# Window scores of an attention layer: whole-array products against products on quarters of TensorE, with keys laid out by two multiplications

## The chip, the cores and the metric

The kernel runs on one core of a Trainium2 chip. The metric is device time in microseconds (us) of one launch. The core's engines are TensorE (PE; its weight loads are shown apart as PEld), VectorE (DVE), ScalarE (ACT), GpSimd (POOL) and SyncE (SP, which issues DMAs). They run side by side, each through its own list of instructions in order, and wait for one another by semaphores. PE writes its products to PSUM, which has eight banks of 128 partitions by 512 float32 values; DVE and ACT read them from there.

## The reference

16 images become 441 tokens each and get 128 text tokens appended, so there are 16 sequences of 569 tokens with 256 features. Layer 0 is an attention in windows of 64 tokens and a mixture of eight experts, layer 1 a phasor attention and an LSTM. Everything is float32. The change touches the window attention alone:

```python
    qkv = xw @ w_qkv.T + b_qkv
    qkv = qkv.reshape(b, w, p, 3, N_HEADS, HEAD_DIM)       # p = 64, 8 heads of 32
    ...
    sim = jnp.einsum('bwphd,bwqhd->bhwpq', q, k) * scale
    ...
    sim = sim + rel_pos[:, idx][None, :, None]
    ...
    probs = jax.nn.softmax(sim, axis=-1)
    out = jnp.einsum('bhwpq,bwqhd->bwphd', probs, v)
    ...
    out = out @ w_out.T + b_out
```

## The kernel before, in words

The program runs in stages. The first holds the tokenizer, the window attention, the norms and the routing of tokens to experts; then come the experts (line 1320 and on), layer 1 and the LSTM, and the output.

The first stage takes the sequences in eight pairs. A pair has nine chunks of 128 rows, each of two windows of 64 tokens (one window of each sequence), so there are 72 chunks. A chunk goes through `windows` (lines 716 to 836) in one of four slots, each slot with a PSUM bank and SBUF tiles of its own. Its steps are: turn the normalised rows (L724); project to queries and keys into the slot's bank, four blocks of 128x128 (L734); add the bias to the queries (L743); lay out the keys (L708); scores (L752); scale and add the relative position (L758); project the values and the gate (L768, L777); softmax (L782 to L803); turn the probabilities (L807); multiply by the values (L819); project out (L830); add to the residual (L832). Then `sent_rows` and `norm` write the normalised rows for the experts. Beside the windows run `features` and `projections` (the tokenizer's input), two slots of `tokens` (its attention, L611 to L652), `norms` (the norm ahead of the windows), and `routing`, which for each pair ranks the experts, counts places by a product with a triangular matrix (L893, L895, into bank 7), and forks `send`, POOL's indirect DMAs (L927). The last pair is routed in three parts: chunks 0 to 3, 4 to 6, and 7 and 8.

How the scores work: the projected keys have 128 partitions, four heads of 32 features each, in two groups m. To get separate scores per head from one product, the key tile `KB` is 128 partitions by 256 columns per window, with head r's keys in columns 64r to 64r + 63 of partitions 32r to 32r + 31 and zeros elsewhere (zeroed once, L445). Four copies per chunk fill in the diagonal blocks (L708: rows 0 and 1 by ACT, 2 and 3 by DVE). A product of 64 queries with 256 columns then gives four heads' scores. For the two windows w it writes the two halves of the output partitions, that is, it uses the array as two halves of 64 columns.

The order of the work is not left to a scheduler. Every step of these generators names its engine and an expected duration (`yield "PE", 0.44, "64"`), and `Order.run` merges the streams: it keeps a clock for each engine, and takes the step that could start earliest. A third entry "64" says that the step uses the array in 64-column tiles; going to another kind is charged. `yield "at", event` holds a stream until another has marked the event; `yield "lock", name` until no other stream holds that name; `first.fork` starts a new stream. The merged order is the order in each engine's list. So a changed duration can move any later instruction of the stage.

Of the kernel before, what the change touches and what calls it, by code (L numbers as in the profile page):

```python
# [297 lines left out]
def kernel(ctx: ExitStack, tc: tile.TileContext, a: dict, out: bass.AP):  # L298
# [121 lines left out]
    def setup():  # L420
# [22 lines left out]
        nc.gpsimd.memset(zeros, 0.0)  # L443
        for t in KB + VB:
            nc.gpsimd.memset(t, 0.0)  # L445
        for t in QT:
            nc.vector.memset(t, 0.0)
        nc.gpsimd.memset(ones, 1.0)
        nc.gpsimd.memset(before, 0.0)
        for e in range(1, E):  # L450
# [149 lines left out]
    def tokens(slot):  # L600

        last = NIMG - 384
        for n in range(slot, 7 * NP, 2):
# [4 lines left out]
            for m in range(2):  # L608
                yield "PE", 0.76, "64"
                for s in range(2):  # L610
                    nc.tensor.matmul(  # L611
                        sc[64 * s : 64 * s + 64, :NIMG], QT[s][:, m, 64 * c : 64 * c + 64],
                        fTs[2 * p + s][:, m, :], start=(m == 0), stop=(m == 1),
                    )
# [20 lines left out]
            for t in range(4):  # L635
                m = min(128, NIMG - 128 * t)
                yield "PE", 0.44, "64"
                for s in range(2):
                    nc.tensor.matmul(
                        mm[64 * s : 64 * s + 64, :], PT[:m, t, 64 * s : 64 * s + 64],  # L640
                        TV[s][:m, t, :], start=(t == 0), stop=(t == 3),
                    )
# [14 lines left out]
    def norm(h, to, name, slot):  # L657

        st = wk.tile([128, 6], F32, name=f"{name}_st", tag=f"st{slot}", bufs=1)
        yield "DVE", 0.43  # L660
        nc.vector.bn_stats(st, h[:, :D])
        mv = wk.tile([128, 2], F32, name=f"{name}_mv", tag=f"mv{slot}", bufs=1)
        yield "DVE", 0.18
        nc.vector.bn_aggr(mv, st)
        rstd = wk.tile([128, 1], F32, name=f"{name}_rstd", tag=f"rstd{slot}", bufs=1)
        yield "POOL", 0.85 if name[0] == "r" else 1.28
        over = mv[:, 1:2]
        nc.gpsimd.tensor_scalar(over, over, EPS, None, ALU.add)
        nc.gpsimd.tensor_tensor(rstd, over, mhalf[:, :1], ALU.pow)
        if name[0] == "w":  # L670
            nc.gpsimd.tensor_tensor(h[:, D + E :], over, half, ALU.pow)
        yield "DVE+", 0.5
        nc.vector.tensor_scalar(to, h[:, :D], mv[:, 0:1], rstd, ALU.subtract, ALU.mult)
        return rstd

    def norms():
# [10 lines left out]
    def sent_rows(p, c, h, slot):  # L687

        if p not in XN:
            if p > 1:  # L690
                yield "at", ("sent", p - 2)
            if p not in XN:
                LG[p] = wk.tile([128, NC, E], F32, name=f"LG{p}", tag="LG", bufs=2)
                XN[p] = xnp.tile([128, NC, WIDE], F32, name=f"XN{p}", tag="XN", bufs=2)
                yield "POOL", 0.2
                nc.gpsimd.tensor_copy(XN[p][:, :, D], cols[:, COL["row"] + NC * p : COL["row"] + NC * (p + 1)])
        rstd = yield from norm(h, XN[p][:, c, :D], f"r{p}_{c}", slot)
        yield "DVE", 0.19
        nc.vector.scalar_tensor_tensor(
            LG[p][:, c, :], h[:, D : D + E], rstd, frow("gate_b", E), ALU.mult, ALU.add  # L700
        )
        first.mark(("normed", p, c))

    def half_of_keys(u, kb, qk, rows, engine):
        for r in rows:
            own = slice(32 * r, 32 * r + 32)
            yield engine, 0.4
            (nc.scalar.copy if engine == "ACT" else nc.vector.tensor_copy)(  # L708
                kb[own, :, :, r, :], qk[own, 1].rearrange("p m (w x) -> p m w x", w=2)
            )  # L710
        first.mark(("keys", u, engine))

    def windows(slot):

        kb, vb = KB[slot], VB[slot]
        for n in range(slot, NC * NP, WINDOWS):
# [13 lines left out]
            for m in range(2):  # L730
                for j in range(2):
                    for k in range(2):
                        yield "PE", 0.25
                        nc.tensor.matmul(  # L734
                            qk[:, j, m, :], wqkv[:, k, D * j + 128 * m : D * j + 128 * m + 128],
                            xT[:, k, :], start=(k == 0), stop=(k == 1),
                        )
            q = wk.tile([128, 2, 128], F32, name=f"wq{u}", tag=f"wq{slot}", bufs=1)
            first.fork(half_of_keys(u, kb, qk, (0, 1), "ACT"))
            first.fork(half_of_keys(u, kb, qk, (2, 3), "DVE"))  # L740
            for m in range(2):
# [5 lines left out]
            yield "at", ("keys", u, "DVE")  # L747
            sc = place_of(f"wsc{u}", slot).rearrange("p (h x) -> p h x", h=NH)
            for m in range(2):
                yield "PE", 0.44, "64"  # L750
                for w in range(2):
                    nc.tensor.matmul(  # L752
                        sc[64 * w : 64 * w + 64, 4 * m : 4 * m + 4, :],
                        q[:, m, 64 * w : 64 * w + 64], kb[:, m, w, :, :], start=True, stop=True,
                    )
            S = wk.tile([128, NH, 64], F32, name=f"wS{u}", tag=f"wS{slot}", bufs=1)
            yield "DVE", 0.69
            nc.vector.scalar_tensor_tensor(  # L758
                S, sc, 32 ** -0.5, relm if c == 8 else rel, ALU.mult, ALU.add
            )  # L760

# [11 lines left out]
            for k in range(2):  # L773
                yield "PE", 0.06, "64"
                for w in range(2):
# [6 lines left out]
            nc.vector.tensor_reduce(top, S, AX.X, ALU.max)  # L782
            yield "DVE", 0.2
            nc.vector.scalar_tensor_tensor(
                h[:, D : D + E], vg[:, D : D + E], h[:, D + E :], win_b[:, D:], ALU.mult, ALU.add
            )
            for odd in range(2):
                own = slice(64 * odd, 64 * odd + 64)
                yield "ACT", 0.4
                nc.scalar.copy(  # L790
# [47 lines left out]
    def routing():  # L838

        for p, lo, hi in PARTS:  # L840
# [45 lines left out]
            for c in range(n):  # L886
                yield "DVE", 0.19
                nc.vector.tensor_tensor(
                    ahead[:, c + 1, :], ahead[:, c, :], both[:, c, :], ALU.add
                )  # L890
            pos = place_of(f"pos{u}", 7)[:, : (n + 1) * E].rearrange("p (c e) -> p c e", e=E)
            yield "PE", 0.3
# [8 lines left out]
            yield "DVE", 0.16  # L901
            nc.vector.tensor_tensor(place0, place0, pos[:, n:, :], ALU.add)
            part = wk.tile([128, 2, n, E], F32, name=f"part{u}", tag="part", bufs=1)
            for of, to in ((pr, share), (place, slot)):
# [32 lines left out]
    with tc.manual_schedule(engines=ENGINES):  # L937
# [8 lines left out]
        win_b = hp.tile([128, D + E], F32, name="win_b")  # L946
        half = hp.tile([128, 1], F32, name="half")
        mixed = hp.tile([128, NB, 2, len(EDGES)], F32, name="mixed")
        QT = [hp.tile([128, 2, 448], F32, name=f"tQ{s}") for s in range(2)]


        KB = [hp.tile([128, 2, 2, 4, 64], F32, name=f"KB{i}") for i in range(WINDOWS)]
        VB = [hp.tile([128, 2, 4, 2, 32], F32, name=f"VB{i}") for i in range(WINDOWS)]
# [1214 lines left out]
```

## Time and profile before

| | us |
|---|---|
| median of 3 runs | 3315.19 |
| lowest and highest run | 3311.05, 3320.17 |
| the profiled execution, its own time | 3305.14 |
| its span, from the first to the last instruction | 3303.4 |
| first score product of the first stage (L752) | starts 59.1 |
| first product of the experts (L1320) | starts 966.8 |

A row of the groups reads: line, engine, operation, output tile <- input tiles, partitions by elements, count | busy us, mean ns of one | idle us of the engine just before them, and what ended most of it. A row of the timeline reads: start, length, engine, line, operation, tiles, shape, count, and in brackets the idle time before it with its releaser. In a shape such as 128\*64 the first number is the rows of the array that a matmul uses and the second its columns; what follows are partitions and columns of the moving data. A float32 matmul of the program is two in the profile. PE's busy time overlaps within itself, as matmuls are pipelined and their ends are modelled; the distance between starts tells what one costs.

### The profile page before, as it was taken

The page shows a single profiled execution, that of the slowest core. Times are in us where ns is not written, and L with a number is a line of the kernel's source. Part 1 is how long each engine was busy: PE and PEld are TensorE (multiplying, and loading weights), DVE is VectorE, ACT ScalarE, POOL GpSimd, SP SyncE. Part 2 cuts the span into 40 slices and gives each one's busy share as a digit, 9 for nine tenths or more (in the row PEclk, how much of TensorE's full clock was granted, in tenths as well). Part 3 has the DMA queues.
Part 4 walks back from the last instruction along what each step waited for, and adds up shares of the span by engine and source line. Part 5 has one row for each costly group of instructions (what it writes and reads, how often), then busy time and mean ns, then how long its engine had stood idle before and what let it go on. Part 6 is the DMA issues. An engine that isn't in the chain of part 4 may idle for free.

```text
span 3303.4 us, 133968 instructions
## 1 busy us (share of the span) xinstructions
PE 2989.9 (91%) x57598; PEld 2205.3 (67%) x57598; DVE 2051.8 (62%) x6946; ACT 1486.8 (45%) x5068; POOL 815.6 (25%) x1579
## 2 busy tenths in 40 slices
PE   6999999999849999997899999999999999899884
PEld 3666666666638888885576767677676766666552
DVE  4678777786742222222676777677777777676555
ACT  3544544454412222222554556556665656454442
POOL 1354465545533332322311101010110010000000
PEclk8999999999979999998999999999999999999997
DMA  5111221101177676773433333333333333233323
GB/s 180 58 62 57 74 85 63 52 31 45 41 240 247 242 254 236 250 245 121 125 89 102 89 91 96 99 92 98 92 88 97 89 100 87 74 96 92 101 86 116
DMA packets 268419, 378.43 MB, mean 115 GB/s; under 512 B 133088, under 2 KB 207888, under 8 KB 255152
## 3 DMA queue, kind: packets, MB, share of 16 engines
q1 hardware_dynamic: 242192, 313.73, 30.1%
q0 software_dynamic: 14160, 38.83, 3.1%
q10 hardware_dynamic: 11472, 17.30, 1.8%
q8 instruction: 451, 7.39, 0.9%
q14 instruction: 144, 1.18, 0.1%
HBM read 252.06 MB, written 117.70 MB: 112 GB/s over the span
## 4 chain that ended last, share of the span: by engine, by line
PE 36%; DVE 7%; ACT 6%; DMA 2%; issue 2%; POOL 0%; SPq 0%; ACTq 0%; DVEq 0%; POOLq 0%
PE gates L1832 13%; PE xm_False L1116 6%; PE out_gate L1841 2%; PE v L1116 2%; ACT act L1853 1%; PE ek L1116 1%; PE eq L1116 1%; ACT th L1889 1%; DMA xo<-XOD 1%; PE r_False L1116 1%; DVE ab L1868 1%; PE po_False L1116 1%; DVE cT L1881 1%; PE ds_False L1116 1%; DVE act L1874 1%
## 5 line engine op out<-in xcount | busy, mean ns | idle before, releaser
L1832 PE MATMUL gates<-W_hh,X 128*16 128x96 f32 (+1 forms) x18176 | 490.8, 248 | 63.9 <-DVE X L1896 60.3
L1832 PEld LDWEIGHTS gates<-W_hh,X 128*16 128x16 f32 (+1 forms) x18176 | 378.3, 103 | 252.9 <-DVE X L1896 236.1
L1327 ACT ACTIVATE hT<-hp,w 128x256 f32<-128x256 f32 (+1 forms) x332 | 132.9, 453 | 448.8 <-PE hp L1320 342.0
L1853 ACT ACTIVATE act<-gates 128x96 f32<-128x96 f32 x568 | 142.1, 250 | 412.1 <-PE gates L1832 403.4
L1116 PE MATMUL xm_False<-W_ih,dxT_False 128*32 128x256 f32 x4352 | 294.3, 382 | 0.8 <-ACT dxT_False L1356 0.6
L1868 DVE SCALAR_TENSOR_TENSOR ab<-act 128x64 f32<-128x64 f32 x568 | 127.9, 225 | 255.6 <-ACT act L1853 248.5
L1334 PE MATMUL y<-w,hT 128*128 128x256 f32 x1208 | 276.3, 381 | 6.9 <-ACT hT L1327 6.8
L1340 DVE TENSOR_TENSOR ys<-y,w 128x512 f32<-128x512 f32 (+1 forms) x83 | 53.4, 644 | 358.5 <-PE y L1334 306.6
L1320 PE MATMUL hp<-xt,w 128*128 128x256 f32 (+1 forms) x1328 | 275.2, 360 | 0.0
L1775 PEld LDWEIGHTS <-nil 128*32 128x32 bf16 x4552 | 186.4, 95 | 119.0 <-issue 60.4
L1334 PEld LDWEIGHTS y<-w,hT 128*128 128x128 f32 x1208 | 226.3, 190 | 41.8 <-ACT hT L1327 11.8
L1320 PEld LDWEIGHTS hp<-xt,w 128*128 128x128 f32 x1328 | 232.8, 190 | 28.7 <-ACT hT L1327 0.2
L1261 POOL DMA_INDIRECT YT<-ys,to x151 | 147.3, 975 | 416.8 <-DVE ys L1340 389.6
L1841 PE MATMUL out_gate<-W_hh,X 128*32 128x64 f32 x9088 | 235.5, 220 | 6.1 <-issue 3.2
L1781 ACT COPY gates<-xc 128x96 f32<-128x96 f32 x569 | 138.6, 244 | 140.9 <-PE gates L1775 62.8
L1841 PEld LDWEIGHTS out_gate<-W_hh,X 128*32 128x32 f32 x9088 | 189.2, 111 | 11.0 <-issue 4.0
L1896 DVE SCALAR_TENSOR_TENSOR X<-toT,th 128x32 f32<-128x32 f32 x569 | 109.6, 193 | 129.2 <-ACT th L1889 126.3
L1889 ACT ACTIVATE th<-cT 128x32 f32<-128x32 f32 x569 | 130.4, 229 | 89.5 <-DVE cT L1881 49.0
L927 POOL DMA_INDIRECT XS<-XN,at x144 | 150.3, 1044 | 51.3 <-issue 24.6
L734 PE MATMUL wqk<-wxT,wqkv 128*128 128x128 f32 x1152 | 150.3, 280 | 7.6 <-ACT wxT L728 7.2
L734 PEld LDWEIGHTS wqk<-wxT,wqkv 128*128 128x128 f32 x1152 | 140.0, 192 | 24.1 <-ACT wxT L728 13.5
L1775 PE MATMUL gates<-nil 128*32 128x96 bf16 x2276 | 132.5, 209 | 24.2 <-ACT act L1853 4.5
(383 smaller groups left out, 6493.8 us busy)
## 6 DMA issues: line engine op xcount, KB each, us to landing
w<-in_wpack SPq DMA_DIRECT2D x83, 1154.0 KB
taps<-in_taps SPq DMA_DIRECT2D x16, 1764.0 KB
xc<-XCD SPq DMA_DIRECT2D x71, 384.0 KB
XCD<-xp_False SPq DMA_DIRECT2D x136, 192.0 KB
yg<-YT SPq DMA_DIRECT2D x72, 256.0 KB
xo<-XOD SPq DMA_DIRECT2D x71, 256.0 KB
xs<-XS SPq DMA_DIRECT2D x68, 258.0 KB
HD<-h SPq DMA_DIRECT2D x72, 128.0 KB
```

Source lines behind the costliest of these rows:

```text
L734: nc.tensor.matmul(qk[:, j, m, :], wqkv[:, k, D * j + 128 * m : D * j + 128 * m + 128], xT[:, k, :], start=(k == 0), stop=(k == 1),)
L927: fill(0, nc.gpsimd.indirect_dma_start(out=XS[0], out_offset=bass.IndirectOffsetOnAxis(ap=at[:, i, c - lo : c - lo + 1], axis=0), in_=XN[p ...
L1116: nc.tensor.matmul(out[own], lhsT[:, own], rhs, start=start, stop=stop)
L1261: keep(nc.gpsimd.indirect_dma_start(out=YT, out_offset=bass.IndirectOffsetOnAxis(ap=to[:, i : i + 1], axis=0), in_=ys[:, i, :], in_offset= ...
L1320: nc.tensor.matmul(hp[:, i, : 128 * n], w1[:, k, hc * 128 : (hc + 1) * 128], xT[:, k, :], start=(k == 0), stop=(k == 1),)
L1334: nc.tensor.matmul(y[:, i, :], hT[:, hc, 128 * i : 128 * i + 128], w2[:, hc, :], start=(hc == 0), stop=(hc == 3),)
L1775: nc.tensor.matmul(g[32 * q : 32 * q + 32, :n], nil[:, :32], nil[:, :n], start=True, stop=last)
L1832: nc.tensor.matmul(GC[32 * q : 32 * q + NB * (1 + half), :96], before[:, kk, NB * (1 - half) :], Whh[:, kk, own : own + 96], start=False, ...
L1841: nc.tensor.matmul(GO[32 * q : 32 * q + 32, :64], before[:, kk, :], Whh[:, kk, own : own + 64], start=False, stop=(kk == 1),)
L1853: nc.scalar.activation(act[:, :96], GC[:, :96], AF.Tanh, scale=0.5), begun.pop((k, t))
L1868: nc.vector.scalar_tensor_tensor(ab, act[:, :64].rearrange("p (g x) -> p g x", g=2), 1.0, act[:, 64:].rearrange("p (g x) -> p g x", g=2), ...
L1889: nc.scalar.activation(th.rearrange("p k x -> p (k x)"), cT, AF.Tanh, scale=0.5)
```

## The change

The key tile has 128 columns per window in place of 256. A pair of heads in 64 partitions shares them: head 2r in columns 0 to 63, head 2r + 1 in columns 64 to 127. A new tile `pairs` holds, in column i, ones in the partitions of heads with parity i and zeros elsewhere. The keys are laid out by two multiplications over all 128 partitions, one by ACT (an activation with `pairs[:, 0]` as scale) and one by DVE (with `pairs[:, 1]`), which write the zeros too; `KB` isn't zeroed beforehand.

The scores become products of 64 partitions (r picks the half) by 64 queries (w picks the output half) with 128 columns, eight per chunk in place of four. The two halves r go to two PSUM banks: the slot's own, and bank 7 for r = 1, which all slots and the routing share under the lock "other scores". The scaling is two instructions of 256 elements in place of one of 512, the one that reads bank 7 first; then the lock is let go.

Beside this, POOL's power for the gate's factor in `norm` becomes a stream of its own (`deviation`), the statistics tile `mv` of `norms` gets three buffers in place of one, and a number of the planner's durations are set anew.

```diff
-        for t in KB + VB:
+        for t in VB:
             nc.gpsimd.memset(t, 0.0)
...
+        for r in range(4):
+            for i in range(2):
+                nc.gpsimd.memset(pairs[32 * r : 32 * r + 32, i : i + 1], float(r % 2 == i))
...
-                yield "PE", 0.76, "64"
+                yield "PE", 0.745, "64"
...
-                yield "PE", 0.44, "64"
+                yield "PE", 0.46, "64"
...
-        mv = wk.tile([128, 2], F32, name=f"{name}_mv", tag=f"mv{slot}", bufs=1)
+        mv = wk.tile([128, 2], F32, name=f"{name}_mv", tag=f"mv{slot}", bufs=3 if slot == "w" else 1)
...
-        yield "POOL", 0.85 if name[0] == "r" else 1.28
+        yield "POOL", 0.9
...
         if name[0] == "w":
-            nc.gpsimd.tensor_tensor(h[:, D + E :], over, half, ALU.pow)
-        yield "DVE+", 0.5
+            first.fork(deviation(h, over))
+        yield "DVE+", 0.46
...
+    def deviation(h, over):
+        yield "POOL", 0.6
+        nc.gpsimd.tensor_tensor(h[:, D + E :], over, half, ALU.pow)
...
-            own = slice(32 * r, 32 * r + 32)
-            yield engine, 0.4
-            (nc.scalar.copy if engine == "ACT" else nc.vector.tensor_copy)(
-                kb[own, :, :, r, :], qk[own, 1].rearrange("p m (w x) -> p m w x", w=2)
-            )
+            yield engine, 0.46 if engine == "ACT" else 0.53
+            own_keys = qk[:, 1].rearrange("p m (w x) -> p m w x", w=2)
+            if engine == "ACT":
+                nc.scalar.activation(kb[:, :, :, r, :], own_keys, AF.Identity, scale=pairs[:, r : r + 1])
+            else:
+                nc.vector.tensor_scalar(kb[:, :, :, r, :], own_keys, pairs[:, r : r + 1], None, ALU.mult)
...
-                        yield "PE", 0.25
+                        yield "PE", 0.225
...
-            first.fork(half_of_keys(u, kb, qk, (0, 1), "ACT"))
-            first.fork(half_of_keys(u, kb, qk, (2, 3), "DVE"))
+            first.fork(half_of_keys(u, kb, qk, (0,), "ACT"))
+            first.fork(half_of_keys(u, kb, qk, (1,), "DVE"))
...
-            sc = place_of(f"wsc{u}", slot).rearrange("p (h x) -> p h x", h=NH)
+            yield "lock", "other scores"
+            sc = [place_of(f"wsc{u}_{r}", (slot, 7)[r])[:, :D].rearrange("p (m x) -> p m x", m=2) for r in range(2)]
             for m in range(2):
-                yield "PE", 0.44, "64"
-                for w in range(2):
-                    nc.tensor.matmul(
-                        sc[64 * w : 64 * w + 64, 4 * m : 4 * m + 4, :],
-                        q[:, m, 64 * w : 64 * w + 64], kb[:, m, w, :, :], start=True, stop=True,
-                    )
+                yield "PE", 0.27, "64"
+                for r in range(2):
+                    two = slice(64 * r, 64 * r + 64)
+                    for w in range(2):
+                        nc.tensor.matmul(
+                            sc[r][64 * w : 64 * w + 64, m, :], q[two, m, 64 * w : 64 * w + 64],
+                            kb[two, m, w, :, :], start=True, stop=True,
+                        )
             S = wk.tile([128, NH, 64], F32, name=f"wS{u}", tag=f"wS{slot}", bufs=1)
-            yield "DVE", 0.69
-            nc.vector.scalar_tensor_tensor(
-                S, sc, 32 ** -0.5, relm if c == 8 else rel, ALU.mult, ALU.add
-            )
+            for r in (1, 0):
+                yield "DVE", 0.43
+                own_heads = [
+                    t.rearrange("p (m r i) x -> p m r (i x)", m=2, r=2)[:, :, r]
+                    for t in (S, relm if c == 8 else rel)
+                ]
+                nc.vector.scalar_tensor_tensor(
+                    own_heads[0], sc[r], 32 ** -0.5, own_heads[1], ALU.mult, ALU.add
+                )
+                if r:
+                    first.unlock("other scores")
...
+            yield "lock", "other scores"
             pos = place_of(f"pos{u}", 7)[:, : (n + 1) * E].rearrange("p (c e) -> p c e", e=E)
...
+            first.unlock("other scores")
...
+        pairs = hp.tile([128, 2], F32, name="pairs")
...
-        KB = [hp.tile([128, 2, 2, 4, 64], F32, name=f"KB{i}") for i in range(WINDOWS)]
+        KB = [hp.tile([128, 2, 2, 2, 64], F32, name=f"KB{i}") for i in range(WINDOWS)]
```

Four more planned durations change in the same way: the gate product (0.06 to 0.087), the gate's DVE step (0.2 to 0.22), the copy of the values (0.4 to 0.47), and the experts' logits (0.19 to 0.25).

More of the change, by code (lines that the diff above doesn't have):

```diff
@@ L697, in sent_rows @@
         rstd = yield from norm(h, XN[p][:, c, :D], f"r{p}_{c}", slot)
-        yield "DVE", 0.19
+        yield "DVE", 0.25
         nc.vector.scalar_tensor_tensor(
@@ L773, in windows @@
             for k in range(2):
-                yield "PE", 0.06, "64"
+                yield "PE", 0.087, "64"
                 for w in range(2):
@@ L782, in windows @@
             nc.vector.tensor_reduce(top, S, AX.X, ALU.max)
-            yield "DVE", 0.2
+            yield "DVE", 0.22
             nc.vector.scalar_tensor_tensor(
@@ L788, in windows @@
                 own = slice(64 * odd, 64 * odd + 64)
-                yield "ACT", 0.4
+                yield "ACT", 0.47
                 nc.scalar.copy(
```

## The prediction

> **What bounds the kernel now.** The diff touches only the first of the kernel's stages. The order in which instructions are built says the same: from the last routing of that stage on, both kernels issue the same instructions on every engine. So I read, in this order: the busy time by stretch, to see where that stage lies and which engine fills it; the groups of its lines; the timeline of TensorE, for the price of one group; and the timeline of the stage's end.
>
> The stretches (columns: us, then PE, PEld, DVE, ACT, POOL busy with counts, granted clock, DMA share, GB/s):
>
> ```profile
> 80.00:880.00 800.00, 746.52 (x6854) 528.81 (x6852) 603.50 (x1629) 386.56 (x1055) 416.14 (x733) 1.00 0.17 57
> 880.00:967.00 87.00, 37.40 (x316) 29.05 (x315) 50.48 (x197) 18.33 (x49) 37.40 (x66) 0.69 0.47 157
> ```
>
> The reader is to see that PE is busy for 93% of the stage's body and DVE for 75%; ACT and POOL are at half. The body ends when PE's work ends, with DVE as the next limit. After 880 the stage runs out, and the experts' first product waits till 966.8. The groups of the body that the change touches (busy us, mean ns | idle before, releasers):
>
> ```profile
> L752 PE MATMUL wsc<-KB,wq 128*64 128x256 f32 x518 | 69.6, 387 | 3.8 <-DVE KB L708 2.2 <-ACT KB L708 0.9 <-ACT wq L743 0.7
> L708 DVE COPY KB<-wqk 32x256 f32<-32x256 f32 x130 | 55.3, 426 | 59.0 <-ACT KB L708 26.0 <-ACT wq L743 22.5 <-PE wqk L734 8.5
> L708 ACT COPY KB<-wqk 32x256 f32<-32x256 f32 x130 | 47.0, 361 | 56.0 <-PE wqk L734 39.4 <-DVE KB L708 15.4
> L758 DVE SCALAR_TENSOR_TENSOR wS<-wsc,rel 128x512 f32<-128x512 f32 x58 | 39.8, 688 | 17.9 <-PE wsc L752 17.0
> ```
>
> Two things stand here. The scores are 70 us of PE. And DVE and ACT wait for each other before the key copies: the readers of one qk bank come one after another, though each copy takes only 0.36 to 0.43 us.
>
> **PE, the scores.** One chunk's scores and what follows, from PE's timeline (start, length, ..., instructions; a float32 product is two):
>
> ```profile
> 315.32 1.03 PE L752 MATMUL wsc<-KB,wq 128*64 128x256 f32 x8
> 316.18 1.76 PE L639 MATMUL tav<-tV,tPT 128*64 128x256 f32 x12
> 317.77 1.04 PE L768 MATMUL wv<-wqkv,wxT 128*64 128x128 f32 x16
> 318.65 0.35 PE L777 MATMUL wv<-gw,wxT 128*64 128x8 f32 x8
> ```
>
> The starts give the price. Eight score instructions, in pairs on the two column halves, are four rounds: 316.18 - 315.32 = 0.86 us, 0.216 us a round of 256 columns. The 16 of L768 are eight rounds of 128 columns: 318.65 - 317.77 = 0.88 us, 0.110 us a round. After the change a chunk has 16 score instructions of 128 columns on 64 rows by 64 columns of the array. If the four quarters run side by side, that is four rounds of 0.110 = 0.44 us. It saves 0.86 - 0.44 = 0.42 us, over 72 chunks **30 us**.
>
> Whether they do, no row shows: no work of the body puts different rows to work at once. The nearest is four column strips, L1116 on the page:
>
> ```profile
> L1116 PE MATMUL xm_False<-W_ih,dxT_False 128*32 128x256 f32 x4352 | 294.3, 382 | 0.8 <-ACT dxT_False L1356 0.6
> ```
>
> 4352 x 0.382 = 1662 us of instructions lie in 294 us, 5.6 deep, where the two halves of L752 are 518 x 0.387 / 69.6 = 2.9 deep. Four tiles at once are thus taken as fast as two, and I take the quarters likewise. The other end is that the two row halves take turns: eight rounds of 0.110 = 0.88 us, no gain.
>
> **PE, the changes of shape.** Of the 12 instructions at 316.18 four have 57 rows, so the array goes to a 64-row shape and back inside the group. Six rounds of 0.216 are 1.30; the group took 317.77 - 316.18 = 1.59. Each change costs (1.59 - 1.30) / 2 = **0.147 us**. In the order of PE's instructions up to the experts I counted changes between the shapes 128x128, 128x64 and 64x64: 349 before, 463 after. The new scores are 64x64, and stand in 79 groups mostly between products on 128x64, which the old ones joined for nothing. The planner counts both as one kind. 114 x 0.147 = **17 us** are given back. Net PE: -30 + 17 = **-13** us.
>
> The Trainium skill, "TensorEngine Tiling (Array Packing)", section Tiling Modes, Key Properties, speaks against the change here: a change of tiling mode, unlike a change of tile, drains the engine. It has no price, so by the rule alone the gain would stand at 30 us less something; by the row it is 13. The same list says that tiles work independently, which would put the quarters side by side; no row here shows that for row tiles.
>
> **DVE and ACT.** Per chunk DVE loses two key copies (2 x 0.426) and one score reading of 512 elements (0.688), 1.54 us in all. It gains one key multiplication of 256 elements from PSUM and two score readings of 256. Neither stands in the trace. For the multiplication the ends are 0.41 (L673, a tensor_scalar of 256 from SBUF, median) and 0.48 (L652, 128x256 from PSUM with a scalar column, median); for a half reading 0.34 (half of 0.688) and 0.48 (L652). I take 0.45 for each, nearer to L652, which reads PSUM: 1.35. DVE: -0.19 a chunk (ends -0.45 and -0.10), -14 us. ACT loses 2 x 0.361 and gains one activation of 256: between 0.365 (L743, 128 elements) and 0.628 (L796, 512), taken as 0.40 near L728's copy of 256 (0.369); -0.3 a chunk, off the path. And six readers of the bank (four copies, two for q) become four: of the 48.5 us that DVE idled before its copies for ACT's readers some 20 should go.
>
> So DVE is blocked for 34 us less of about 650 (603 busy and those 48), 5%; PE for 13 less of 747, 2%. PE has 53 us of idle in the body, much of it waiting for DVE and ACT. Were DVE alone the limit, the body would lose 5% of 800, 42 us. I take PE's 13 in full and **6 us** more; the ends of the latter are 0 and 42 - 13 = 29.
>
> **What the other edits cost.** One bank (7) now serves the second half of the scores of all four slots and the routing's positions, under a lock. Held from the score's turn on PE to the first DVE reading, it is some 0.5 + 0.45 us of work and as much again of waiting for turns, 2 to 4 us, 72 + 10 times: a quarter of the stage. A second chunk then waits 1 to 2 us in one case of four, about 0.5 us a chunk. Four slots take 72 chunks, each 18. From the first transpose (44.8) to the last wob (928) a slot's turn is 883 / 18 = 49 us, while the last chunk alone took 902.2 to 928.7, 26.5 us. So the wait is covered, and I take **1 us**; without the cover it is 18 x 0.5 = 9. Queued behind a score that waits for bank 7 is all of PE's later work, and the engines that read it. The lock makes the planner place a score after the earlier reading, so PE stands only where DVE runs late; the like wait of L768 for the reading of its own bank costs 5.1 us in the body, and comes sooner after it. The POOL power moved into its own step (L671, 0.58 us) is the same work; DVE's normalisation waits for L669 ahead of it in either case. The triple mv lets bn_aggr run ahead, which it never waited to do. The eight small memsets for pairs and the four of KB that go (0.94 each) lie on POOL before 8 us, and POOL's next work starts at 42.2 after 34 us of idle: nothing. The planner's new durations move no work by themselves; they make another order, whose luck I bound from the profile: the seven whole routings' products L893 start at 204.0, 307.8, 422.4, 539.7, 637.5, 747.0, 840.1; against an even 106 us they stray by up to 18 us, and most by less than 10. I take **+-10 us**.
>
> **The end of the stage** is a chain:
>
> ```profile
> 926.53 2.13 PE L830 MATMUL wob<-wout,wAT 128*128 128x264 f32 x4 [0.53 <-ACT wAT L826]
> 935.36 0.62 PE L893 MATMUL pos<-ahead,ones 128*128 128x24 f32 x2 [6.71 <-DVE ahead L888]
> ...
> 961.95 2.79 PE L1290 MATMUL xtr<-ident,xs 128*128 128x128 f32 x12 [25.55 <-DMA xs<-XS]
> ```
>
> Before, the routing of chunks 4 to 6 was done (921.1) ahead of the last wob. In the new order it stands behind it, and DVE does some 20 of its small instructions (0.07 to 0.41 us, here at 915 to 924.6) between the last chunk's residual and its own routing: **+4 us** (0 to 7). POOL's six sends for it, 1.27 us apart, end about when the last routing does, so they hide or add 1.
>
> **Sum.** -13 - 6 + 1 + 4 = **-14**. The profiled execution took 3305.1 (span 3303.4 and 1.7 around it), so it would become 3291. It lies 10 below the median of the runs, 3315.2, the base of the forecast: **3301**.
>
> **Rivals.**
> 1. *The forecast* (0.52): quarters side by side, shape changes paid, 3291 to 3311 with the order's luck.
> 2. *DVE was the limit* (0.16): the freed readings and turns shorten the body beyond PE's part. Against it: PE is 18 points busier. -13 - 29 + 5 = -37: 3278.
> 3. *The plan eats it* (0.15): the lock uncovered (+9), a longer end (+7), an unlucky order (+10), against -19: some +7 at worst, 3311 to 3326, centre 3316, no difference.
> 4. *Slower: the row halves take turns on the array* (0.17). Then 72 x (0.86 - 0.88) = -1 is saved, and 17 of shape changes are paid: +18, +5 for lock and end, -6 of DVE's relief, +17: 3332. It decides from 0.19 us a chunk lost of the 0.42 (14 / 72), and shows in a measurement from 0.33; for it speaks that no row has row tiles, against it the four strips of L1116. That the change doesn't do what it says is this case too.
>
> A measurement here tells about 0.3%, 10 us, from no change. Faster by that: three quarters of the first case, and the second, 0.39 + 0.16 = 0.55. Within: 0.13 + 0.12 = 0.25. Slower: the fourth and the worst of the third, 0.20. The range takes in most of cases 2 and 4: 3276 to 3328.
>
> **What would show it.** Right: the score's 16 instructions start in rounds of four, a chunk's scores take 0.44 to 0.55 us between starts, 0.09 to 0.15 us appears around each 64x64 group, DVE's idle before the key line falls from 59 to 30 or 40, and the experts' first product comes at about 952 instead of 966.8. Wrong: rounds of two (case 4); PE busy well below 90% in the body with DVE waiting on the lock (case 3); a body shorter by over 25 us (case 2).

## The result, and the profile after

| us | before | after |
|---|---|---|
| median of six runs each | 3316.76 (3311.05 to 3324.33) | **3293.18** (3288.29 to 3298.29) |
| the profiled execution, its own time | 3305.14 | 3288.29 |
| its span | 3303.4 | 3286.4 |
| first product of the experts starts | 966.8 | 950.4 |
| from there to the end of the span | 2336.6 | 2336.0 |

The ratio of the medians is 0.9928, with a 95% interval of 0.9913 to 0.9944: faster by 24 us. The forecast was 14 less than before. The profile puts 16.4 of its 17.0 us into the first stage, as it should, since nothing behind that stage was changed. The other 7 us between 17 and 24 can't be placed: over the single profiled executions of all the kernels here, the part behind the first stage, with the same instructions, took 2327.8 to 2342.9 us, so two profiled executions can differ there by up to 15 us without any change.

The stretches of the kernel after (columns as before: us, then PE, PEld, DVE, ACT, POOL busy with counts, granted clock, DMA share, GB/s):

```profile
80.00:880.00 800.00, 740.61 (x7429) 525.44 (x7426) 575.87 (x1643) 368.86 (x990) 432.92 (x744) 0.99 0.17 58
880.00:967.00 87.00, 43.31 (x346) 36.13 (x345) 43.56 (x189) 18.22 (x49) 32.47 (x58) 0.74 0.54 182
```

PE is filled as before (740.6 of 800 against 746.5), although its work became less; the same window holds a little more of the stage. DVE fell by 28 us and ACT by 18. The groups that were changed, from 100 to 880 us (busy us, mean ns of one | idle before, releasers):

```profile
L763 PE MATMUL wsc<-KB,wq 64*64 64x128 f32 x1040 | 45.6, 285 | 0.4 <-issue 0.3
L718 DVE TENSOR_SCALAR KB<-wqk,pairs 128x256 f32<-128x256 f32 x65 | 31.0, 481 | 50.8 <-ACT KB L716 34.6 <-PE wqk L742 6.5 <-ACT wq L751 4.7
L716 ACT ACTIVATE KB<-wqk,pairs 128x256 f32<-128x256 f32 x66 | 31.4, 476 | 54.1 <-PE wqk L742 50.6 <-PE wtr L732 1.7 <-DVE KB L718 1.6
L774 DVE SCALAR_TENSOR_TENSOR wS<-wsc,rel 128x256 f32<-128x256 f32 x117 | 46.8, 419 | 40.3 <-PE wsc L763 24.6 <-PE tav L642 5.3 <-PE wob L848 4.2
```

Three things are to be seen. The scores are 45.6 us of PE where they were 69.6, and 1040 x 0.285 = 296 us of instructions lie in them, 6.5 deep. They wait 0.4 us in all, and their weight loads 17.6, where they waited 22.5 before:

```profile
L752 PEld LDWEIGHTS wsc<-KB,wq 128*64 128x64 f32 x512 | 32.7, 136 | 22.5 <-ACT KB L708 4.7 <-issue 3.8 <-ACT wq L743 1.4
L763 PEld LDWEIGHTS wsc<-KB,wq 64*64 64x64 f32 x1040 | 28.3, 133 | 17.6 <-issue 8.8 <-ACT tPT L636 1.8 <-ACT wq L751 1.7
```

The reading of bank 7 (L774) is not among the releasers, so the lock is not seen to cost anything in this execution. And DVE's keys cost 31.0 + 50.8 = 81.8 us with the idle time before them, where they cost 55.3 + 59.0 = 114.3: mostly it is the busy part that went, while the idle part fell by 8 (by 4 in a second execution of the same kernel, after_again below, 55.4).

How a chunk's scores now run, from PE's timeline:

```profile
303.46 0.67 PE L763 MATMUL wsc<-KB,wq 64*64 64x128 f32 x16
304.06 1.09 PE L786 MATMUL wv<-wqkv,wxT 128*64 128x128 f32 x16
```

The 16 instructions take 304.06 - 303.46 = 0.60 us to the next group's start, the median of the whole groups too. In single instructions they start four at a time, 0.109 us a round; four rounds are 0.44, and the remaining 0.16 are the change of shape: the next group's start is 0.10 to 0.11 us late, and the first round of a new shape is 0.053 us longer. The stage's end:

```profile
907.68 1.16 PE L848 MATMUL wob<-wout,wAT 128*128 128x264 f32 x4 [1.14 <-ACT wAT L844]
912.30 0.41 PE L912 MATMUL pos<-ahead,ones 128*128 128x32 f32 x2 [3.46 <-DVE ahead L906]
912.54 0.56 PE L914 MATMUL pos<-both,strict 128*128 128x24 f32 x2
918.59 0.59 PE L912 MATMUL pos<-ahead,ones 128*128 128x24 f32 x2 [5.48 <-DVE ahead L906]
...
943.16 2.79 PE L1311 MATMUL xtr<-ident,xs 128*128 128x128 f32 x12 [23.57 <-DMA xs<-XS]
949.49 1.12 PE L1311 MATMUL xtr<-ident,xs 128*128 128x128 f32 x4 [3.53 <-DMA xs<-XS]
950.40 3.19 PE L1341 MATMUL hp<-xt,w 128*128 128x256 f32 x7
```

Two routings now stand behind the last wob (912.3 and 918.6), where there was one. The last wob starts at 908.5, and from there to the experts it is 41.9 us; before it was 966.8 - 928.0 = 38.8. So the body gained some 19.5 us, and the end gave 3.1 back. The end, too, depends on the order: over the kernels below it took 39.3 to 43.5 us.

### The profile page after: what moved, and what is told of

It reads as the page before. It is cut to its first block, busy times and chain, and to the rows that moved or that the text cites. A ratio compares the mean times of both kernels' runs of the same rounds, so it can differ in the third digit from the quotient of the medians.

```text
span 3286.4 us, 135034 instructions
## 1 busy us (share of the span) xinstructions
PE 2974.4 (91%) x58174; PEld 2193.6 (67%) x58174; DVE 2017.0 (61%) x6946; ACT 1468.9 (45%) x4996; POOL 824.8 (25%) x1583
## 4 chain that ended last, share of the span: by engine, by line
PE 38%; DVE 7%; ACT 5%; issue 2%; DMA 1%; POOL 0%; SPq 0%; ACTq 0%; DVEq 0%; POOLq 0%
PE gates L1853 13%; PE xm_False L1137 6%; PE out_gate L1862 2%; PE v L1137 2%; PE ek L1137 2%; PE r_False L1137 2%; PE eq L1137 1%; ACT act L1874 1%; ACT th L1910 1%; PE po_False L1137 1%; PE ds_False L1137 1%; DVE ab L1889 1%; DVE cT L1902 1%; DVE X L1917 1%; DVE act L1895 1%
## 5 line engine op out<-in xcount | busy, mean ns | idle before, releaser
L1853 PE MATMUL gates<-W_hh,X 128*32 128x96 f32 (+1 forms) x18176 | 490.0, 248 | 65.6 <-DVE X L1917 61.7
L1853 PEld LDWEIGHTS gates<-W_hh,X 128*32 128x32 f32 (+1 forms) x18176 | 377.5, 103 | 255.6 <-DVE X L1917 235.6
L1403 POOL TENSOR_SCALAR d_False_rstd<-d_False_mv 128x2 f32<-128x2 f32 (+1 forms) x36 | 8.9, 247 | 584.4 <-DVE d_False_mv L1395 305.2
```

The source lines that it names most:

```text
L1853: nc.tensor.matmul(GC[32 * q : 32 * q + NB * (1 + half), :96], before[:, kk, NB * (1 - half) :], Whh[:, kk, own : own + 96], start=False, ...
```

## The experiments

Two theories were to be told apart. **The first** is the prediction's: PE is the limit of the body, so each microsecond that its list gets shorter is a microsecond of time, and the keys add a little. **The second**: the body is limited as much by the readers of the qk bank. ACT and DVE read it in turn, each keeping to its own list's order, so what the layout of the keys takes shows in the time, and PE's time shows only in part.

The runs were made on three chips, one for each group below; the kernel before was run beside each group (medians 3309.8, 3311.7 and 3321.6). So ratios compare across groups, and microseconds within one. "First expert product" is its start in the profile, one execution each.

### First group: what PE's time is worth

**after_again** is the changed kernel once more, as the base of this group.

> The changed kernel once more, as the base for the kernels beside it, which keep its order of instructions: a ratio to the kernel before of 0.991 to 0.995, the experts' first product at about 950 us.

Measured: 3286.1 us, ratio 0.9933 (0.9915 to 0.9952); first expert product at 953.5. It repeats the result.

**whole_rows** takes the quarters back and keeps all else, the order too. Each product contracts all 128 partitions, so its scores mix the two halves' heads; only its time is of use.

```diff
-    sc[r][64 * w : 64 * w + 64, m, :], q[two, m, 64 * w : 64 * w + 64],
-    kb[two, m, w, :, :], start=True, stop=True,
+    sc[r][64 * w : 64 * w + 64, m, :], q[:, m, 64 * w : 64 * w + 64],
+    kb[:, m, w, :, :], start=True, stop=True,
```

> Only the score products change: each works on all 128 rows of the array and sums both halves' pairs of heads, so the scores are wrong; number, columns, banks, every other instruction and the order stay. Shape changes on PE: 342 in place of 463. Theory (the gain is PE's, the quarters run side by side): a chunk's scores cost 0.88 us in place of 0.44, +32 us, less 121 x 0.147 = 18 us of shape changes, so +14 us against the changed kernel: 3307, first expert product at about 964. Rival 1 (the gain is DVE's and ACT's, from fewer key instructions): no difference, 3293. Rival 2 (the row halves take turns): -18 us, 3275.

Measured: 3295.8 us, ratio 0.9953 (0.9936 to 0.9969). The group of the scores from 100 to 880 us, and where the experts begin:

```profile
L763 PE MATMUL wsc<-KB,wq 128*64 128x128 f32 x1050 | 71.6, 276 | 0.2 <-issue 0.2
```

```profile
958.50 1.00 PE L1341 MATMUL hp<-xt,w 128*128 128x256 f32 x2
```

The scores cost PE again what they did in the kernel before (71.6 us against 69.6), and 121 of the 463 shape changes are gone. Net, PE pays 72 x 0.44 - 121 x 0.155 = 13 us more than after, and the time is 9.7 longer. But it is still 14 us under the kernel before, with PE's score bill unchanged and nearly as many shape changes (342 against 349). That part of the gain didn't come from PE's scores; it came from the keys and the readings or from the order, which is another than the kernel before has and which the later groups show to be worth as much.

**half_products** also leaves out the products with r = 1, so that a chunk has four rounds in place of eight; both readings take the same values.

```diff
...
-            sc = [place_of(f"wsc{u}_{r}", (slot, 7)[r])[:, :D]... for r in range(2)]
+            sc = [place_of(f"wsc{u}", slot)[:, :D]...] * 2
...
-                for r in range(2):
-                    two = slice(64 * r, 64 * r + 64)
+                for r in range(1):
...
```

> As the kernel with whole rows, but with half of its products: one set in the slot's bank, which both readings of DVE take, so half the scores are left out and the rest are wrong. PE's time for the scores is 0.44 us a chunk as with quarters running side by side, without their shape changes (342 in place of 463). Theory: 121 x 0.147 = 18 us below the changed kernel, 3275, and 32 us below the kernel with whole rows, if PE's time counts in full. Rival (PE's time is hidden, DVE and ACT are what counts): 3293 as both.

Measured: 3282.3 us, ratio 0.9912 (0.9894 to 0.9929).

```profile
L762 PE MATMUL wsc<-KB,wq 128*64 128x128 f32 x540 | 44.0, 279 | 0.1
```

```profile
941.02 1.06 PE L1340 MATMUL hp<-xt,w 128*128 128x256 f32 x2
```

Against whole_rows, which has the same order and the same shapes, 72 x 0.44 = 32 us of PE are gone. The time fell by 13.5 and the experts came 17.5 earlier: PE's time counts for 0.42 to 0.55 of itself (one execution each in the profile, six and seven in the medians). This pair is the cleanest measure of it here.

**no_short_rows** removes the shape changes that the tokenizer's products with 57 rows cause, by zero-filled rows; the scores stay quarters.

```diff
...
-                m = min(128, NIMG - 128 * t)
...
-                        mm[64 * s : 64 * s + 64, :], PT[:m, t, 64 * s : 64 * s + 64],
-                        TV[s][:m, t, :], start=(t == 0), stop=(t == 3),
+                        mm[64 * s : 64 * s + 64, :], PT[:, t, 64 * s : 64 * s + 64],
+                        TV[s][:, t, :], start=(t == 0), stop=(t == 3),
```

> The changed kernel with the tokenizer's last 57 rows filled up with zeros to 128, so that those products stay in the shape of their neighbours; same order. Shape changes 387 in place of 463. Theory (each change costs 0.147 us of the engine that ends the stage): 76 x 0.147 = -11 us, 3282, first expert product at about 939. Rival (changes of shape fall into waiting and cost nothing): 3293.

Measured: 3283.9 us, ratio 0.9921 (0.9903 to 0.9939); first expert product at 950.7. 76 changes fewer, 387, are about 12 us of PE; the time fell by 2 to 3 us, not clear of the noise. With whole_rows, whose 13 us of PE came to 5 (in the profile) to 10 (in the medians), this is the second theory's side: over the three pairs PE's microsecond is worth 0.2 to 0.75 of one, about half, and not all of it.

### Second group: what the keys are worth

**four_copies** lays out the keys by four copies of 32 partitions again, in the new tile and in the changed kernel's order, with the quarters kept.

```diff
-        for t in VB:
+        for t in KB + VB:
             nc.gpsimd.memset(t, 0.0)
...
-            own_keys = qk[:, 1].rearrange("p m (w x) -> p m w x", w=2)
-            if engine == "ACT":
-                nc.scalar.activation(kb[:, :, :, r, :], own_keys, AF.Identity, scale=pairs[:, r : r + 1])
-            else:
-                nc.vector.tensor_scalar(kb[:, :, :, r, :], own_keys, pairs[:, r : r + 1], None, ALU.mult)
+            for of in (2 * r, 2 * r + 1):
+                own = slice(32 * of, 32 * of + 32)
+                (nc.scalar.copy if engine == "ACT" else nc.vector.tensor_copy)(
+                    kb[own, :, :, of % 2, :], qk[own, 1].rearrange("p m (w x) -> p m w x", w=2)
+                )
```

> The changed kernel with its new scores, but the keys laid out by four copies as before (two by ACT, two by DVE, on 32 partitions each; KB zeroed once), in place of the two multiplications; every other instruction and the order stay. DVE has 72 x (2 x 0.426 - 0.481) = 27 us more work, ACT 72 x (2 x 0.361 - 0.476) = 18 us more, and six readers of the bank take turns in place of four. Theory after the runs with the score products (PE's time counts about half, the rest of the gain is DVE's and ACT's relief): +8 to +14 us against the changed kernel, first expert product at 959 to 966. Rival 1 (PE's part is all, as the prediction's sum had it): +6. Rival 2 (the rest of the gain is the order's luck or the other edits): no difference, 950 to 954.

Measured: 3331.2 us, ratio 1.0057 (1.0041 to 1.0073): slower than the kernel before, and the experts start at 996.1, 43 us later than in after_again. That is far above what was expected. The groups from 100 to 880 us:

```profile
L716 DVE COPY KB<-wqk 32x256 f32<-32x256 f32 x126 | 53.7, 426 | 57.7 <-ACT KB L716 36.4 <-ACT wq L751 10.0 <-PE wqk L742 5.1
L716 ACT COPY KB<-wqk 32x256 f32<-32x256 f32 x126 | 45.4, 360 | 52.9 <-PE wqk L742 47.9 <-issue 2.0 <-DVE KB L716 2.0
```

DVE's keys cost 53.7 + 57.7 = 111.4 us with their idle time, against 81.8. The idle rows name who waits: DVE for ACT's keys (36.4), ACT for PE's projection, one after the other on one bank. ACT's bias for the queries, which reads the same bank, waits for DVE's keys in turn; its idle time grew from 29.6 to 50.8 us (after, then four_copies):

```profile
L751 ACT ACTIVATE wq<-wqk,cols 128x128 f32<-128x128 f32 x130 | 45.7, 370 | 29.6 <-DVE KB L718 26.8 <-issue 1.5 <-DVE r_mv L667 0.9
L751 ACT ACTIVATE wq<-wqk,cols 128x128 f32<-128x128 f32 x126 | 44.5, 369 | 50.8 <-DVE KB L716 49.8 <-PE wav L837 0.6
```

In a chunk this chain is longer by 2 x 0.426 - 0.481 on DVE and 2 x 0.360 - 0.476 on ACT, 0.62 us together; over 72 chunks 44 us, and the time shows 41 to 43. So in this order the chain goes into the time as if whole, where PE's time goes in by half. That it is this chain, link by link, is argued from the match and the waits; the 43 us that the four copies cost with the order held are measured.

**scores_alone** has the change without its side edits: the planner's old durations, one statistics tile, the power left in `norm`.

```diff
-                yield "PE", 0.745, "64"
+                yield "PE", 0.76, "64"
...
-        mv = wk.tile([128, 2], F32, name=f"{name}_mv", tag=f"mv{slot}", bufs=3 if slot == "w" else 1)
+        mv = wk.tile([128, 2], F32, name=f"{name}_mv", tag=f"mv{slot}", bufs=1)
...
-            first.fork(deviation(h, over))
-        yield "DVE+", 0.46
+            nc.gpsimd.tensor_tensor(h[:, D + E :], over, half, ALU.pow)
+        yield "DVE+", 0.5
```

> The change without its side edits: new keys and scores, but the planner's old durations for all other steps, one mv buffer, and POOL's power inside the norm. Another order follows. Theory (keys and scores make the gain): ratio to the kernel before 0.990 to 0.996, first expert product at 945 to 960. Rival (the new durations and the forked power make the better order): 0.997 to 1.001, 963 to 968.

Measured: 3286.3 us, ratio 0.9928 (0.9913 to 0.9944); first expert product at 948.2. The whole gain is there without the side edits.

**plan_alone** is the other part: the kernel before with those side edits alone (the diff above, the other way round).

> The kernel before with the side edits alone: the new planned durations, three mv buffers, POOL's power as a stream of its own; keys and scores as before. Theory: nothing beyond the order's luck, ratio 0.997 to 1.003, first expert product at 957 to 977. Rival (the side edits carry the part that isn't PE's): 0.993 to 0.997, 950 to 958.

Measured: 3310.8 us, ratio 0.9996 (0.9984 to 1.0008); first expert product at 972.4. The side edits are not seen to be worth anything, in the one order that they make here.

**other_order** makes another order of the same instructions. One planned duration moves by 0.01, and the gate's step waits for the deviation's mark.

```diff
-            first.fork(deviation(h, over))
+            first.fork(deviation(name, h, over))
...
+        first.mark(("deviation", name))
...
+            yield "at", ("deviation", f"w{u}")
...
-            yield "ACT", 0.63
+            yield "ACT", 0.64
```

> The changed kernel in another order of the same instructions: one planned duration 0.01 us longer (the exponential, 0.63 to 0.64), and the gate's step also held till POOL's power has been placed. Theory (an order is worth some +-10 us of luck, as the forecast had it): a first expert product between 940 and 962. Rival (the changed kernel's order is a lucky one): 962 or later.

Measured: 3299.3 us, ratio 0.9960 (0.9946 to 0.9974); first expert product at 965.8. So 9 us of 24 (0.9960 against 0.9933 in the first group) can go by the order alone. The start lies in the rival's range, which said that the changed kernel's own order is a lucky one; third_order below speaks against that.

### Third group: orders of their own

**quarters_with_copies** asks whether four_copies was so slow because its order was made for two multiplications. It is scores_alone with four copies, each planned as a step of its own.

```diff
...
-            yield engine, 0.46 if engine == "ACT" else 0.53
-            own_keys = qk[:, 1].rearrange("p m (w x) -> p m w x", w=2)
...
+            own = slice(32 * r, 32 * r + 32)
+            yield engine, 0.4
+            (nc.scalar.copy if engine == "ACT" else nc.vector.tensor_copy)(
+                kb[own, :, :, r % 2, :], qk[own, 1].rearrange("p m (w x) -> p m w x", w=2)
+            )
...
```

> The new scores alone, planned for: keys laid out by the four copies of before (two steps of 0.4 us on each engine, KB zeroed once), all durations but those of the scores and their readings as before, one mv buffer, POOL's power inside the norm. Changes of shape on PE: 474. Theory after the runs so far (the key stage of a chunk is worth 0.6 us on the path and carries most of the gain; the scores on quarters are worth some 6 us when their changes of shape are paid): ratio 0.996 to 1.000, first expert product at 957 to 968. Rival (the quarters make the gain, and the 42 us of the four copies in the changed kernel's order came from steps that were not planned for): 0.991 to 0.995, 945 to 955.

Measured: 3343.9 us, ratio 1.0072 (1.0057 to 1.0087), slower than both the theory and the rival had it. The shape changes of its order are 477.

```profile
L711 DVE COPY KB<-wqk 32x256 f32<-32x256 f32 x124 | 52.8, 426 | 59.4 <-ACT KB L711 29.7 <-ACT wq L746 19.4 <-PE wqk L737 6.7
```

```profile
999.91 1.06 PE L1336 MATMUL hp<-xt,w 128*128 128x256 f32 x2
```

An order of its own doesn't help: the copies cost the same 52.8 + 59.4 us on DVE, and the time is 1.0072 - 0.9928 = 1.4%, 48 us, above scores_alone. Quarters without the multiplications don't make the kernel faster: here it is 22 to 24 us slower than the kernel before, and 7 slower than before_other_order, which follows, so how much of that is the order's luck stays open.

**third_order** and **before_other_order** are one more order of each kernel. In the changed kernel the residual's planned duration moves from 0.42 to 0.43, with the same mark as in other_order; in the kernel before, one planned ACT copy moves from 0.59 to 0.61.

```diff
-            yield "DVE", 0.42
+            yield "DVE", 0.43
```

```diff
-            yield "ACT", 0.59
+            yield "ACT", 0.61
```

> The changed kernel in a third order of the same instructions: the residual's planned duration 0.43 in place of 0.42, and the gate's step held till POOL's power has been placed. Theory (luck of +-10 us about a mean gain of some 17 us): first expert product between 945 and 966. Rival (the orders of the changed kernel that ran so far were lucky): 962 or later.

> The kernel before in another order: the copy of the turned probabilities planned at 0.61 us in place of 0.59. Theory (the order's luck is the same size here, and the kernel before was not an unlucky draw): first expert product between 957 and 977. Rival (it was an unlucky draw): below 957.

Measured: third_order 3289.1 us, ratio 0.9901 (0.9887 to 0.9916), first expert product at 952.2; before_other_order 3337.1 us, ratio 1.0037 (1.0023 to 1.0051), first expert product at 994.5, outside of what was expected. Of the three orders of the kernel before, its own is among the better two. Three orders of the changed kernel lie between 0.990 and 0.996 (some 20 us), three of the kernel before (plan_alone is one) between 0.9996 and 1.0037 (some 14 us): the sign stands in every pair of the orders tried, the size doesn't.

**kinds_planned** is no_short_rows with the planner told of the third shape: the scores are one step of a kind of its own, with 0.15 for a change.

```diff
-TO_TILES = {None: 0.0, "all": 0.0, "32": 0.11, "64": 0.15}
-FROM_TILES = {None: 0.0, "all": 0.0, "32": 0.18, "64": 0.19}
+TO_TILES = {None: 0.0, "all": 0.0, "32": 0.11, "64": 0.15, "quarter": 0.15}
+FROM_TILES = {None: 0.0, "all": 0.0, "32": 0.18, "64": 0.19, "quarter": 0.19}
...
+            yield "PE", 0.44, "quarter"
...
-                yield "PE", 0.27, "64"
```

> The changed kernel with the tokenizer's last 57 rows filled up to 128, the scores as one step of 0.44 us, and the planner told that products on quarters are a kind of their own, a change to or from it charged at 0.15 us. Changes of shape 389 in place of 463, no score group split. Theory (PE's time counts about half): 74 x 0.147 = 11 us less of PE, -5 us, and order's luck: first expert product at 938 to 958. Rival (planning for the changes matters more than their number): below 938.

Measured: 3292.8 us, ratio 0.9908 (0.9893 to 0.9924); first expert product at 953.7, in the theory's range. With third_order it is the best ratio here, but its interval meets that of after_again (0.9915 to 0.9952), so it isn't shown to beat the changed kernel.

## Why the prediction was right, and where not

**The sum: the sign right, the size near, and partly by luck.** 14 less was forecast and 24 less was measured; the likeliest case (3291 to 3311) holds 3293, near its lower end. Two terms of the sum were mis-sized against each other, as said below, and another order of the same instructions could have made it 9 us more (other_order) or some 10 less (third_order).

**PE's scores: right.** Eight instructions' 0.86 us became four rounds of 0.109. The rows of four strips, from which it was carried over, told the truth for quarters. *Rival 4*, halves that take turns, is out: rounds of four stand in the trace, the group is 6.5 deep.

**The shape changes: right.** 0.147 us was taken from the group with 57 rows; 0.155 was measured around the new groups. 463 of them were counted ahead, and no_short_rows shows that they can be removed for little gain.

**"I take PE's 13 in full and 6 us more": this is the step that failed.** Both halves of it were mis-sized, and against each other. PE's time counts for about half (half_products against whole_rows), so its 13 us are 5 to 10 (whole_rows against after_again, in the profile and in the medians). And the keys with the readings are not 6: about 14 by whole_rows against the kernel before, though an order's luck is as large as that, and more by the copies put back, 43 us in the same order and 48 in an order of its own. *Rival 2*, that DVE is the limit, didn't come true by its own sign (a body shorter by over 25 us; it was 19.5), but it had more of the mechanism than its 0.16 says. What misled was the share of busy time: PE at 93% looked like the limit. As I read it now, PE's list passes in order through chunks that wait for the qk bank, so a shorter group on PE partly moves up a wait; that reading is argued, the half is measured. The idle time before DVE's key copies stood in the lines shown and was counted, 20 us of it, but behind PE's 13 only 6 us were let through; the 56 before ACT's copies were taken as hidden.

**"DVE's idle before the key line falls from 59 to 30 or 40": wrong.** It fell to 50.8. Fewer readers don't wait less: DVE has one turn in place of two, but waits for ACT's longer reading (34.6 us against 26.0). Its waits for ACT's readers together fell from 48.5 to 39.3 (34.6 + 4.7), 9 us where 20 was taken. What shrank most was the work. The prices were 0.481 for DVE's multiplication (0.45 taken), 0.419 for a half reading (0.45), 0.476 for ACT's (0.40): DVE -0.22 us a chunk, 16 us in all where 14 was taken, and ACT -0.25 a chunk, 18 us, which was called "off the path" and, by four_copies, is on it.

**The lock: covered, as taken.** One microsecond was taken; in the changed kernel's profile no idle time before the scores can be charged to it. In other_order some can, 2.0 us before the scores and 2.3 before their weight loads, both for the reading (L775 there):

```profile
L764 PE MATMUL wsc<-KB,wq 64*64 64x128 f32 x1048 | 47.1, 286 | 2.7 <-DVE wS L775 2.0 <-ACT KB L717 0.4 <-DVE KB L719 0.3
L764 PEld LDWEIGHTS wsc<-KB,wq 64*64 64x64 f32 x1048 | 28.7, 133 | 18.6 <-issue 7.8 <-ACT wAT L846 3.2 <-DVE wS L775 2.3
```

*Rival 3* loses that part, the 9 us of an uncovered lock; its other part, an unlucky order, is real in size: other_order takes 9 us of the gain, the three orders of the changed kernel span some 20 us and those of the kernel before some 14. The +-10 was fair, and the lines shown don't tell on which side of it the two kernels lie.

**The end of the stage: right.** +4 was taken and +3.1 measured, by the same chain: a routing more behind the last wob, then POOL's sends, then the experts' rows.

**Side edits at nothing: right as far as seen** (plan_alone, 0.9996; scores_alone, 0.9928 without them).

**What stays open.** With copies, quarters are slower than whole rows (1.0057 and 1.0072 against 0.9996 to 1.0037); with multiplications in the same order, they are faster (0.9933 against 0.9953), though other_order, at 0.9960, is not faster than whole_rows. So the parts don't add up: quarters and multiplications are each worth more beside the other. Part of that may be the luck of the orders, of which there are one to four for each pairing, and the runs can't divide it. Nor do they settle why the readers' chain counts whole in four_copies, although four slots could cover it; that the slots cover less than all is what the time says, but no view here shows the slots' turns one by one.

## What to carry to other kernels

Where engines run hand-ordered lists, a busy share of 93% doesn't make an engine's microsecond worth one: weigh it against the chains that the other engines walk in order, and add up busy and idle time of the readers of one PSUM bank, since they come one after another. A bank's readers are to be counted by instructions and their lengths, not by bytes; half the readers over all the partitions beat twice as many over a quarter of them each (0.9933 against 1.0057 in one order). When a change moves a planned order, try one part in the same order and again in an order of its own: two orders of the same instructions differed by up to some 20 us here, nearly as much as the change is worth.

## What the runs showed of the hardware

- Four quarters of 64 rows by 64 columns take float32 products side by side, four instructions of 128 columns starting every 0.109 us. The Trainium skill, "TensorEngine Tiling (Array Packing)", section Tiling Modes, Key Properties, says that tiles work independently; these rows agree for row tiles.
- A change between 128\*64 and 64\*64 cost 0.10 to 0.11 us on the next start and 0.053 on the first round.
- An ACT activation with a column as scale, 128x256 from PSUM, took 0.476 us, where a copy of the same size took 0.369 (L728 before); DVE's multiplication by a column took 0.481, where the copy of 32x256 took 0.426. On ACT it isn't the partitions that cost, since the copy of 32x256 took 0.361; another activation with a column, the bias of L751, 128x128, took 0.370 where a copy of 57x128 (L636) took 0.266, so some 0.10 over a copy there too. The runs don't tell the column from the activation itself, nor on DVE the column from the partitions.
- Splitting one DVE reading of 512 elements (0.688 us) into two of 256 (0.419 each) cost 0.15 us.
